# Gate sums, bank reads and first loads around the matmuls of a two-layer graph attention kernel

## The chip, the cores and the metric

The kernel runs on one core of a Trainium2 chip. The metric is device time in microseconds (us), lower is better. PE is the matmul engine, DVE the vector engine, ACT the scalar engine, POOL the general engine, SP the engine that issues most transfers. A "group" is four graphs; there are 32 groups in each of two layers, and they are counted here from 0 to 63.

Names in the traces: `xn` is a group's rows as loaded, `xT` the same rows turned (transposed), `T` POOL's sums of `xT`; `wv`, `wq`, `wk`, `wo` are weights with their sums; `e` is exp(scores), `av` the product of v and e; `aT` and `T_o` are the attention's result, turned, and its sums; `h` is the output before it is stored.

## The reference, cut to what matters

```python
# layer 0, per graph of N = 128 nodes, D = 512, 8 heads; everything is float32
Q, K, V = x @ W_q + b_q, x @ W_k + b_k, x @ W_v + b_v
scores  = Q K^T / sqrt(64) + (a_i + c_j + b_g) + log(adjacency + 1e-9)   # a, c = x @ halves of w_g: the gate sums
x1      = softmax(scores) V + x
# ... x1 is cut and turned into the graphs of layer 1
# layer 1: the same attention without the gate, then
h   = (attention output) @ Wo + bo + x1
out = layer_norm(h) * gamma + beta
```

The kernel never adds the logarithm: it multiplies exp(scores) by the turned adjacency. That product, `e <- e,adjT`, is DVE's largest job: 349.9 us in the trace before.

## The kernel before

Each 512 x 512 product is computed with Strassen's seven products P1 to P7; P2 is itself split by Strassen into four phases (P2.1 to P2.4) from the second group on. A matrix takes seven slots. Matrix n+1 starts while the last units of matrix n ("b") still run:

```python
SLOTS = ("P1", "P2.1"), ("P4 b",), ("P3 b", "P2.2"), ("P6", "P2.3"), ("P5",), ("P7", "P2.4"), ()
```

P2's phases share one PSUM bank, p1, with the next matrix. DVE must have read P2.4 out of p1 before PE may begin the next P2.1:

```python
def inner(phase):                       # P2's phases; DVE reads bank p1 after each
    ...
    else:                               # phase 4, after P7
        add(0, 0, p, v, 1, 3)           # DVE: last read of p1
def unit(i):
    ...
    elif i == "P7":
        kept("u3", p, 1, 1)             # ACT copies P7 out of its bank
        add(1, 1, t["b"], t["u3"])      # DVE adds it, ahead of the last read of p1
```

The rest of the work is hung on slots; `first` is the first slot of the group's matrix v, `put(post, ...)` issues behind the slot's matmuls.

```python
for k, i in enumerate((0, 0, 2, 6, 13, 17, 18, 19)):      # eight gate sums on DVE
    put(post, first + i, gate, t, k // 2, k % 2)
put(post, first + 20, gate_exp, t)
for k in range(2):
    put(post, first + 21 + k, add_row, t, k)               # bias row onto xn, on POOL
# start: xn whole on SP's queue, wv on ACT's queue; four turned graphs, then the sums of wv
for b in range(G):
    transposed(XT[0][:, b], XN[0, b // 2][:, b % 2], ...)   # copies out on ACT, DVE, ACT, DVE
Strassen.combine_outer(nc.vector, WV[0][0])                 # four additions and a negation of wv
# layer 1, end of a group: normalise on ACT, times gamma, plus beta on POOL, store from SP's queue
engine.tensor_tensor(HS[t, n], HS[t, n], wide(BE), ALU.add)
nc.sync.dma_start(out[...], HS[t, n])
```

(Cut: the loads, the attention, the path for unusual inputs, the last group, which works graph by graph.)

## Time and profile before

| | before |
|---|---|
| median of 4 runs | 3261.0 us (3260.05 to 3262.13) |
| span of the profiled run | 3259.4 us |
| PE busy | 3212.7 us, 99% |
| period of a group in layer 0 / layer 1 | 44.44 / 55.79 us |
| last scores to end of span | 44.1 us |

The prediction below shows the lines of the profile and reads them. To read on one needs one habit: a line's first number is its start, the second its duration, and what stands in brackets is how long its engine stood idle before it and for whom. For PE, start to start of the same step is a better measure than the durations: in the trace before, sixteen matmuls at 815.68 are shown 1.90 us long, and the next begin 1.73 us after them. In layer 1 a single group's period can lie up to 1.7 us above the common one, so I read sums over many groups.

### The profile page before, as it was taken

To read this page: it belongs to the slowest core of one execution; us is meant where nothing else is said; L and a number is where in the kernel's file an instruction comes from. 1 tells how busy PE (TensorE), PEld (TensorE's weight loads), DVE (VectorE), ACT (ScalarE), POOL (GpSimd) and SP (SyncE) were. 2 spreads that over 40 slices of the span, in tenths; PEclk is the share of its full clock that TensorE was granted. 3 is DMA by queue.
4 is the path that set the end of the run, shared out by engine and by line. 5 is a ranking of instruction groups with operands and counts; after the bars stand their busy time and mean duration, and the time that the engine had idled before them with its cause. 6 is when DMAs were issued, how large, how long until landed. Compare 5 with 4: busy or idle time off the path is not lost.

```text
span 3259.4 us, 95184 instructions
## 1 busy us (share of the span) xinstructions
PE 3212.7 (99%) x39974; PEld 2358.3 (72%) x39974; DVE 2023.1 (62%) x4070; ACT 1133.6 (35%) x1951; POOL 1806.0 (55%) x1518
## 2 busy tenths in 40 slices
PE   9999999999999999999999999999999999999997
PEld 6777777777777777776777777777777777777774
DVE  6777766777766777764555555555555555555555
ACT  2333333333333333333333333333333333333332
POOL 4444433444433444475676766576676757676765
PEclk9999999999999999999999999999999999999999
DMA  5333333333333333342343434343433334343432
GB/s 124 83 78 83 77 84 67 82 79 82 77 83 68 83 79 82 90 114 46 74 91 75 93 71 97 67 94 69 85 81 75 90 74 93 72 96 70 98 63 72
DMA packets 1017180, 265.82 MB, mean 82 GB/s; under 512 B 942640, under 2 KB 949808, under 8 KB 1016752
## 3 DMA queue, kind: packets, MB, share of 16 engines
q1 hardware_dynamic: 1015408, 258.39, 35.4%
q8 instruction: 319, 5.23, 0.7%
q10 hardware_dynamic: 1088, 1.05, 0.1%
q14 instruction: 109, 0.89, 0.1%
q0 software_dynamic: 256, 0.26, 0.0%
HBM read 159.92 MB, written 67.11 MB: 70 GB/s over the span
## 4 chain that ended last, share of the span: by engine, by line
PE 90%; DVE 5%; SPq 2%; issue 2%; DMA 1%; ACT 0%; POOL 0%; DVEq 0%; ACTq 0%
PE p0q L124 10%; PE p3v L124 9%; PE p3k L124 9%; PE s L124 8%; PE av L124 7%; PE p2v L124 7%; PE p2q L124 7%; PE p0o L124 6%; PE p2k L124 5%; PE p3q L124 3%; PE p2o L124 3%; PE p1v L124 3%; PE p1q L124 3%; PE p0k L124 3%; PE p1k L124 3%; DVE gw L124 2%
## 5 line engine op out<-in xcount | busy, mean ns | idle before, releaser
L124 DVE TENSOR_TENSOR e<-e,adjT 128x1024 f32<-128x1024 f32 x256 | 349.9, 1408 | 144.1 <-ACT e L124 144.1
L124 POOL TENSOR_TENSOR xn<-o,xn 128x1024 f32<-128x1024 f32 x64 | 140.9, 2202 | 455.0 <-DVE o L124 359.4
L124 POOL TENSOR_TENSOR xn<-xn,row 128x1024 f32<-128x1024 f32 x128 | 331.8, 2603 | 13.0 <-DMA xn<-x1d 10.0
L124 DVE SCALAR_TENSOR_TENSOR gw<-xn,gw 128x512 f32<-128x512 f32 x256 | 317.0, 1238 | 1.2
L124 PE MATMUL p3k<-T,wk 128*64 128x256 f32 x2256 | 268.5, 380 | 0.0
L124 PE MATMUL p0q<-T,wq 128*64 128x256 f32 x2256 | 267.4, 379 | 0.0
L124 PE MATMUL p3v<-wv,T 128*64 128x256 f32 x2256 | 267.4, 379 | 0.0
L124 POOL TENSOR_TENSOR T<-xT 128x512 f32<-128x512 f32 x128 | 219.3, 1713 | 84.5 <-DVE xT L124 83.9
L124 POOL TENSOR_TENSOR inner<-xT 128x128 f32<-128x128 f32 x126 | 67.5, 536 | 355.6 <-DMA adjT<-in_adj_dram 241.7
L124 PE MATMUL s<-qT,kT 64*128 64x128 f32 x4096 | 263.1, 278 | 0.0
L124 PE MATMUL av<-v,e 128*64 128x65 f32 x8192 | 260.9, 221 | 0.0
L124 PEld LDWEIGHTS av<-v,e 128*64 128x64 f32 x8192 | 256.6, 137 | 1.0 <-issue 0.8
L124 PEld LDWEIGHTS s<-qT,kT 64*128 64x128 f32 x4096 | 238.6, 188 | 22.4 <-issue 11.7
L124 POOL TENSOR_TENSOR h<-h,gamma 128x1024 f32<-128x1024 f32 x61 | 145.0, 2376 | 128.3 <-ACT h L124 128.2
L124 PEld LDWEIGHTS p3k<-T,wk 128*64 128x64 f32 x2256 | 159.5, 138 | 68.8 <-issue 1.3
L124 PEld LDWEIGHTS p0q<-T,wq 128*64 128x64 f32 x2256 | 159.1, 137 | 67.6
L124 PEld LDWEIGHTS p3v<-wv,T 128*64 128x64 f32 x2256 | 159.0, 137 | 67.7
L124 ACT COPY o<-av 128x520 f32<-128x520 f32 x256 | 151.7, 593 | 130.9 <-PE av L124 116.3
L124 POOL TENSOR_TENSOR h<-h,xn 128x1024 f32<-128x1024 f32 x62 | 146.8, 2390 | 62.1 <-ACT h L124 59.2
L124 DVE STREAM_TRANSPOSE xT<-xT 128x512 f32<-128x512 f32 x252 | 176.5, 701 | 0.5 <-issue 0.5
L124 PE MATMUL p0o<-wo,T_o 128*64 128x256 f32 x1488 | 176.4, 379 | 0.0
L124 DVE TENSOR_TENSOR t1q<-p1q,t1q 128x128 f32<-128x128 f32 x189 | 54.5, 288 | 188.5 <-PE p1q L124 187.4
(229 smaller groups left out, 6643.4 us busy)
## 6 DMA issues: line engine op xcount, KB each, us to landing
xn<-in_x_dram SPq DMA_DIRECT2D x64, 512.0 KB, 4.1
x1d<-xn SPq DMA_DIRECT2D x64, 512.0 KB, 3.0
xT<-x1d SPq DMA_DIRECT2D x512, 64.0 KB, 2.4
xn<-x1d SPq DMA_DIRECT2D x64, 512.0 KB, 6.1
xT<-in_x_dram SPq DMA_DIRECT2D x496, 64.0 KB, 2.6
out_dram<-h SPq DMA_DIRECT2D x62, 512.0 KB, 4.2
aT<-o SPq DMA_DIRECT2D x984, 32.0 KB, 2.0
adjT<-in_adj_dram SPq DMA_DIRECT2D x256, 64.0 KB, 3.5
```

The lines of the kernel that those rows point to most:

```text
L124: return lambda *args, **kw: self.tc.keep_in_program_order(f(*args, **kw))
```

## The change

Its intent: in layer 0, lay DVE's gate sums where POOL rests, so they do not hold up DVE (in the trace before they take 0.65 us at the least and up to 2.73 beside POOL); read p1 before U3 is added; at the start bring xn in quarters and wv over two queues and give PE something to do before; at the change of layers replace 16 matmuls for the output bias by eight weighted sums on DVE and move a turn of aT behind a read of p1; in the last group, work in pairs and let two groups' ends overlap.

```diff
             else:
                 add(0, 0, p, v, 1, 3)
+                add(1, 1, t["b"], t["u3"])
             elif i == "P7":
                 kept("u3", p, 1, 1)
-                add(1, 1, t["b"], t["u3"])
+                if not inside:
+                    add(1, 1, t["b"], t["u3"])
-            for k, i in enumerate((0, 0, 2, 6, 13, 17, 18, 19)):
+            for k, i in enumerate((6, 6, 10, 10, 13, 13, 21, 21)):
-                put(post, first + 21 + k, add_row, t, k)
+                put(post, first + (11, 22)[k], add_row, t, k)
-    load_natural(0)
-    strassen_weights(WV, 0, w_v0, "wv0", nc.scalar)
+    load_natural(0, nc.sync, nc.scalar)
+    strassen_weights(WV, 0, w_v0, "wv0", nc.sync, nc.scalar)
+    (eight matmuls of ones into a free bank)
     for b in range(G):
         transposed(...)
+        if b == 0:
+            Strassen.combine_outer(nc.vector, WV[0][0], 0)     # S1, S2: ahead of DVE's copies
-    Strassen.combine_outer(nc.vector, WV[0][0])
-    put(post, V2 + 17, output_bias)                           # 16 matmuls in the trace
+    put(post, V2 + (10, 10, 13, 13)[c], weigh_rows, c)        # on DVE
+    put(pre, V2 + 17, output_bias)                            # 4 in the trace, against ones
-                turned = f + 18
+                turned = f + (18 if t > NG else 21)
```

(Cut: three slots of the turns and one of the inner sums of xT, one slot of the gates' exponential, the later halves of the sums of wv and wq at the start, the steps of five slots at the change of layers, the last count's move into this list, and the last group's list.)

More of the change, by code (lines that the diff above doesn't have):

```diff
@@ L66, in load, with combine @@
     @staticmethod
-    def load(engine, t, w):
+    def load(engines, t, w):
         q = w.rearrange("(k c p) (m e) -> k m p c e", k=2, p=P, m=2)
-        for (k, m), i in Strassen.RAW.items():
-            engine.dma_start(t[:, i], q[k, m])
+        for n, ((k, m), i) in enumerate(Strassen.RAW.items()):
+            engines[n % len(engines)].dma_start(t[:, i], q[k, m])
     @staticmethod
-    def combine(v, a11, a12, a21, na22, s1, s2, s4):
-        v.tensor_tensor(s1, a21, na22, ALU.add)
-        v.tensor_tensor(s2, s1, a11, ALU.subtract)
+    def combine(v, a11, a12, a21, na22, s1, s2, s4, part=None):
+        if part != 1:
+            v.tensor_tensor(s1, a21, na22, ALU.add)
+            v.tensor_tensor(s2, s1, a11, ALU.subtract)
+        if part == 0:
+            return
         v.tensor_tensor(a21, a11, a21, ALU.subtract)
@@ L82, in combine_outer @@
     @staticmethod
-    def combine_outer(v, t):
+    def combine_outer(v, t, part=None):
         w = Strassen
-        w.combine(v, *(t[:, i] for i in (w.A11, w.A12, w.S3, w.NA22, w.S1, w.S2, w.S4)))
+        w.combine(v, *(t[:, i] for i in (w.A11, w.A12, w.S3, w.NA22, w.S1, w.S2, w.S4)), part)
     @staticmethod
@@ L124, in __getattr__, with fast_path @@
             return lambda *args, **kw: self.tc.keep_in_program_order(f(*args, **kw))
-def fast_path(ctx, tc, args, GOOD):
+def fast_path(ctx, tc, args, GOOD, bad):
     (x, adj, w_q0, b_q0, w_k0, b_k0, w_v0, b_v0, w_g, b_g, w_q1t, b_q1, w_k1t, b_k1, w_v1t, b_v1,
@@ L191, in load, with load_natural @@
             load_graph(t, b, nc.sync)
-    def load_natural(t):
+    def load_natural(t, *engines):
         L, g = split(t)
@@ L197, in load_natural @@
             XN[t, k] = act.tile([P, 2, D], F32, tag="xn", name=f"xn_{t}_{k}", bufs=4)
-            nc.sync.dma_start(XN[t, k], src[2 * k : 2 * k + 2].rearrange("b p d -> p b d"))
+            if not engines:
+                nc.sync.dma_start(XN[t, k], src[2 * k : 2 * k + 2].rearrange("b p d -> p b d"))
+            for b, engine in enumerate(engines):
+                engine.dma_start(XN[t, k][:, b], src[2 * k + b])
     def turn(v):
@@ L516, in stats, with root @@
         nc.vector.bn_aggr(MV[t][:, b], st)
+    def root(t, bs):
+        rs = RS[t][:, 0, bs]
+        nc.gpsimd.tensor_scalar_add(rs, MV[t][:, bs, 1], LN_EPS)
+        nc.gpsimd.tensor_tensor(rs, rs, minus_half[:, bs], ALU.pow)
     def scales(t, bs):
+        root(t, bs)
         mv, rs = MV[t][:, bs], RS[t][:, :, bs]
-        nc.gpsimd.tensor_scalar_add(rs[:, 0], mv[:, :, 1], LN_EPS)
-        nc.gpsimd.tensor_tensor(rs[:, 0], rs[:, 0], minus_half[:, bs], ALU.pow)
         nc.gpsimd.tensor_tensor(rs[:, 1], mv[:, :, 0], rs[:, 0], ALU.mult)
@@ L536, in store, with weigh_rows, strassen_weights @@
         )
-    def output_bias():
-        p = ps.tile([P, 4 * N], F32, tag="p2", name="pbo").rearrange("p (m e) -> p m e", m=2)
-        for m in range(2):
-            for c in range(KC):
-                nc.tensor.matmul(
-                    p[:, m], bvcols[:, c], WO[1][0][:, Strassen.RAW[c // 2, m], c % 2],
-                    start=(m == 0 and c == 0), stop=(c == KC - 1), skip_group_check=True,
-                )
-        r = ROWS[1].rearrange("p (m e) -> p m e", m=2)
-        nc.vector.tensor_tensor(r, p, r, ALU.add)
-    def strassen_weights(to, key, w, name, engine):
+    def weigh_rows(c):
+        for m in range(2):
+            o, w, b = GW[:, 2, m * D2 : (m + 1) * D2], WO[1][0][:, Strassen.RAW[c // 2, m], c % 2], bv1[:, c : c + 1]
+            if c == 0:
+                nc.vector.tensor_scalar(o, w, b, None, ALU.mult)
+            else:
+                nc.vector.scalar_tensor_tensor(o, w, b, o, op0=ALU.mult, op1=ALU.add)
+    def output_bias():
+        p = ps.tile([P, 2, D], F32, tag="s", name="pbo", bufs=2)[:, 0]
+        for half in HALVES:
+            nc.tensor.matmul(p[half], ones[:, half], GW[:, 2], start=True, stop=True, skip_group_check=True)
+        nc.vector.tensor_tensor(ROWS[1], p, ROWS[1], ALU.add)
+    def strassen_weights(to, key, w, name, *engines):
         to[key] = (
@@ L555, in strassen_weights @@
         )
-        Strassen.load(engine, to[key][0], w)
+        Strassen.load(engines, to[key][0], w)
     def combine(engine, w):
@@ L562, in fast_path @@
     load_tiles(0)
-    load_natural(0)
-    strassen_weights(WV, 0, w_v0, "wv0", nc.scalar)
+    load_natural(0, nc.sync, nc.scalar)
+    strassen_weights(WV, 0, w_v0, "wv0", nc.sync, nc.scalar)
+    ones = const.tile([P, P], F32, name="ones")
+    nc.vector.memset(ones, 1.0)
+    busy = ps.tile([P, 4 * N], F32, tag="p0", name="busy")
+    for i in range(4):
+        nc.tensor.matmul(busy[:, 0:N], ones, ones, start=True, stop=True)
     load_adjacency(0, nc.sync)
@@ L578, in fast_path @@
     for b in range(G):
-        transposed(XT[0][:, b], XN[0, b // 2][:, b % 2], f"x_{b}", nc.vector.tensor_copy if b % 2 else nc.scalar.copy, ("p1", "p2")[b % 2])
+        transposed(XT[0][:, b], XN[0, b // 2][:, b % 2], f"x_{b}", nc.vector.tensor_copy if b % 2 else nc.scalar.copy, ("p1", "p2", "p3")[b % 3])
+        if b == 0:
+            Strassen.combine_outer(nc.vector, WV[0][0], 0)
     TS[0] = quarters(XT[0])
-    Strassen.combine_outer(nc.vector, WV[0][0])
     for s in Strassen.SUMS:
@@ L599, in fast_path @@
     BQ[1], BK[1], bv1 = column(nc, const, b_q1, "bq1"), column(nc, const, b_k1, "bk1"), column(nc, const, b_v1, "bv1")
-    bvcols = GW[:, 3].rearrange("p (c e) -> p c e", e=P)
     GA, BE = row(nc, const, gamma, "gamma"), row(nc, const, beta, "beta")
@@ L633, in fast_path @@
         a = slot("k", t, 7)
-        for k in range(2):
-            put(pre, a + (4, 11 if t + 1 < LAST else 9)[k], scores, t, k)
+        step = 5 if t == NG else 7
+        for k in range(2 if t + 1 < LAST else 0):
+            put(pre, a + 4 + step * k, scores, t, k)
             for b in (2 * k, 2 * k + 1):
-                put(pre, a + (4, 11 if t + 1 < LAST else 9)[k], weigh, t, b)
+                put(pre, a + 4 + step * k, weigh, t, b)
             if t + 1 < LAST:
-                put(pre, a + 7 + 7 * k, mix, t, (2 * k, 2 * k + 1))
-                put(post, a + 7 + 7 * k, normalise, t, k)
+                put(pre, a + 7 + step * k, mix, t, (2 * k, 2 * k + 1))
+                put(post, a + 7 + step * k, normalise, t, k)
                 if L == 1:
-                    put(post, a + 8 + 7 * k, move, t, k, [nc.sync, nc.gpsimd] if t == NG and k else [nc.sync])
+                    put(post, a + 8 + step * k, move, t, k, [nc.sync, nc.gpsimd] if t == NG and k else [nc.sync])
         if t + 1 < LAST:
@@ L650, in fast_path @@
                 put(post, first + (-1 if t == 0 else 2 + 7 * (b // 2) * late), load_graph, n, b, nc.sync)
-                put(post, first + ((9, 13, 16, 17), (16, 17, 23, 24))[late][b], lambda n, b: turn(XT[n][:, b]), n, b)
+                put(post, first + ((8, 9, 15, 17), (16, 17, 23, 24))[late][b], lambda n, b: turn(XT[n][:, b]), n, b)
             put(post, first + (11, 16 if t == NG + 1 else 13)[late], load_adjacency, n, nc.sync)
@@ L654, in fast_path @@
             put(post, first + (13, 17)[late], lambda n: TS.update({n: quarters(XT[n])}), n)
-            put(post, first + (13, 17)[late], lambda n: inner_sums(TS[n], n), n)
+            put(post, first + (17, 17)[late], lambda n: inner_sums(TS[n], n), n)
             for s in Strassen.SUMS:
@@ L660, in fast_path @@
                 put(post, first + 17, load_natural, t + 1)
-            for k, i in enumerate((0, 0, 2, 6, 13, 17, 18, 19)):
+            for k, i in enumerate((6, 6, 10, 10, 13, 13, 21, 21)):
                 put(post, first + i, gate, t, k // 2, k % 2)
-            put(post, first + 20, gate_exp, t)
+            put(post, first + 21, gate_exp, t)
             for k in range(2):
-                put(post, first + 21 + k, add_row, t, k)
+                put(post, first + (11, 22)[k], add_row, t, k)
         else:
@@ L682, in fast_path @@
                     put(post, o + 1 + k, residual, t, k)
-                    stat, scaled, end, stored = (
-                        ((2, 6), 6, 9, 10), ((9, 10), 10, 13, 14)
-                    )[k] if t < LAST - 2 else (((3, 3), 3, 4, 5), ((6, 6), 6, 6, 7))[k]
+                    if t == LAST - 2:
+                        continue
+                    stat, scaled, end, stored = (((2, 6), 6, 9, 10), ((9, 10), 10, 13, 14))[k]
                     for b in range(2):
@@ L690, in fast_path @@
                         put(post, o + end, scale, t, 2 * k + b)
-                    put(post, o + stored, store, t, k, nc.vector if t == LAST - 2 and k else nc.gpsimd)
+                    put(post, o + stored, store, t, k, nc.gpsimd)
     V1, V2 = slot("v", NG - 1, 0), slot("v", NG, 0)
@@ L701, in fast_path @@
     put(post, V2 + 10, load_row, 1, b_o1)
-    put(post, V2 + 10, nc.vector.tensor_copy, bvcols, bv1.rearrange("p (c o) -> p c o", o=1).to_broadcast([P, KC, P]))
-    put(post, V2 + 17, output_bias)
+    for c in range(KC):
+        put(post, V2 + (10, 10, 13, 13)[c], weigh_rows, c)
+    put(pre, V2 + 17, output_bias)
     put(post, V2 + 18, lambda: Strassen.combine_outer(nc.gpsimd, WO[1][0]))
     put(post, slot("o", NG, 1), lambda: Strassen.combine_inner(nc.gpsimd, *WO[1]))
-    put(post, 2, lambda: Strassen.combine_outer(nc.vector, WQ[0][0]))
+    put(post, 0, lambda: Strassen.combine_outer(nc.vector, WV[0][0], 1))
+    put(post, 3, lambda: Strassen.combine_outer(nc.vector, WQ[0][0]))
     put(post, 7, turn_adjacency, 0)
@@ L714, in fast_path @@
     t = LAST - 1
-    a = slot("k", t, 11)
+    a = slot("k", t, 7)
     last = {}
@@ L747, in output_one, with begin_one @@
         stats(t, b)
-        rs = RS[t][:, 0, b : b + 1]
-        nc.gpsimd.tensor_scalar_add(rs, MV[t][:, b, 1:2], LN_EPS)
-        nc.gpsimd.tensor_tensor(rs, rs, minus_half[:, b : b + 1], ALU.pow)
-    def finish_one(b):
+        root(t, slice(b, b + 1))
+    def begin_one(t, b):
         h = HS[t, b // 2][:, b % 2]
-        nc.vector.tensor_scalar(h, h, MV[t][:, b, 0:1], RS[t][:, 0, b : b + 1], ALU.subtract, ALU.mult)
-        nc.vector.tensor_tensor(h, h, GA, ALU.mult)
-        nc.vector.tensor_tensor(h, h, BE, ALU.add)
+        nc.vector.scalar_tensor_tensor(h, h, MV[t][:, b, 0:1], GA, op0=ALU.subtract, op1=ALU.mult)
@@ L757, in finish_one @@
+    def finish_one(t, b):
+        h = HS[t, b // 2][:, b % 2]
+        nc.vector.scalar_tensor_tensor(h, h, RS[t][:, 0, b : b + 1], BE, op0=ALU.mult, op1=ALU.add)
         nc.sync.dma_start(out[split(t)[1] * G + b], h)
-    put(post, slot("v", t, 11), plain_weight)
-    put(post, a, prepare)
-    for b, i in enumerate((3, 4, 7, 8)):
-        put(pre, a + i, mix, t, (b,))
-        put(post, a + i, normalise_one, b)
-        put(pre, a + i + 2, transpose_one, b)
-        put(pre, a + i + 3, output_one, b)
-        put(post, a + (9, 9, 11, 12)[b], finish_one, b)
@@ L767, in fast_path, with store_one, sum_good @@
-    put(post, a + 9, count, t)
+    def store_one(t, b):
+        h = HS[t, b // 2][:, b % 2]
+        nc.gpsimd.tensor_tensor(h, h, GA, ALU.mult)
+        nc.gpsimd.tensor_tensor(h, h, BE, ALU.add)
+        nc.sync.dma_start(out[split(t)[1] * G + b], h)
+    def sum_good():
+        good = small.tile([P, 1], F32, name="good_sum", bufs=1)
+        nc.vector.tensor_reduce(good, GOOD, AX.X, ALU.add)
+        last["good"] = ps.tile([P, 4 * N], F32, tag="p1", name="good_total")[0:1, 0:1]
+        nc.tensor.matmul(last["good"], good, ones[:, 0:1], start=True, stop=True)
@@ new lines, in judge @@
+    def judge():
+        nc.vector.tensor_scalar(bad, last["good"], 2 * B * H * P - 0.5, None, ALU.is_lt)
+    put(post, slot("v", t, 11), plain_weight)
+    put(post, a + 4, prepare)
+    u = t - 1
+    for i, f, *of in (
+        (4, scores, t, 0), (4, weigh, t, 0), (4, weigh, t, 1), (8, mix, t, (0, 1)), (9, normalise_one, 0),
+        (9, normalise_one, 1), (9, scores, t, 1), (9, weigh, t, 2), (9, weigh, t, 3), (10, transpose_one, 0),
+        (10, transpose_one, 1), (11, stats, u, 0), (11, stats, u, 1), (11, output_one, 0), (11, scales, u, slice(0, 2)),
+        (12, mix, t, (2, 3)), (12, scale, u, 0), (12, scale, u, 1), (12, store_one, u, 0), (13, normalise_one, 2),
+        (13, normalise_one, 3), (13, stats, u, 2), (13, stats, u, 3), (13, output_one, 1), (13, store_one, u, 1),
+        (14, transpose_one, 2), (14, transpose_one, 3), (14, begin_one, t, 0), (14, finish_one, t, 0),
+        (14, begin_one, u, 2), (14, begin_one, t, 1), (14, finish_one, t, 1), (15, output_one, 2),
+        (15, root, u, slice(2, 4)), (15, begin_one, t, 2), (15, begin_one, u, 3), (15, finish_one, t, 2),
+        (16, output_one, 3), (16, begin_one, t, 3), (16, count, t), (16, sum_good), (16, finish_one, u, 2),
+        (16, finish_one, t, 3), (16, finish_one, u, 3), (16, judge),
+    ):
+        put(pre, a + i, f, *of)
@@ L797, in count_good @@
     )
-def any_bad(ctx, tc, GOOD, n, bad):
-    nc = tc.nc
-    pool = ctx.enter_context(tc.tile_pool(name="sums", bufs=1))
-    ps = ctx.enter_context(tc.tile_pool(name="sums_ps", bufs=1, space=PSUM))
-    good = pool.tile([P, 1], F32, name="sums_good")
-    nc.vector.tensor_reduce(good, GOOD, AX.X, ALU.add)
-    ones = pool.tile([P, 1], F32, name="sums_ones")
-    nc.vector.memset(ones, 1.0)
-    total = ps.tile([1, 1], F32, name="sums_total")
-    nc.tensor.matmul(total, good, ones, start=True, stop=True)
-    nc.vector.tensor_scalar(bad, total, n - 0.5, None, ALU.is_lt)
 def general_path(ctx, tc, args):
@@ L951 @@
     with ExitStack() as inner:
-        fast_path(inner, tc, args, GOOD)
-    with ExitStack() as inner:
-        any_bad(inner, tc, GOOD, 2 * B * H * P, bad)
+        fast_path(inner, tc, args, GOOD, bad)
     again = nc.values_load(
```

## The prediction

> **What bounds the kernel now.** I read the page first, then the table of who waited for whom for the matmul engine, then the starts of its instructions in order of time.
>
> ```profile
> PE 3212.7 (99%) x39974; PEld 2358.3 (72%) x39974; DVE 2023.1 (62%) x4070; ACT 1133.6 (35%) x1951; POOL 1806.0 (55%) x1518
> PEclk9999999999999999999999999999999999999999
> ```
> PE is busy 99% of the span at full clock, so a change that leaves the matmuls as they are can win only the moments in which PE stands still. Of 3259.4 us the page leaves 3259.4 - 3212.7 = 46.7 us. A gain of 2% would be 65 us, so it is nearly ruled out before any detail. The waits of PE say where those moments are:
>
> ```profile
> PE p1v L124 <- DVE kT L124: 13.4, 31, 0.8
> PE po L124 <- ACT aT_last L124: 6.5, 4, 4.4
> PE sums_total L810 <- DVE sums_ones L808: 5.9, 1, 5.9
> PE tr_x L124 <- DMA xn<-in_x_dram: 5.7, 1, 5.7
> PE p1o L124 <- DVE kT L124: 3.4, 1, 3.4
> ```
> The first row is one wait per group of four graphs in layer 0; the rest are single events at the end, the start and the change of layers. The waits understate it, because a matmul's end in the trace is modelled. Starts are better. The same step (P1 into one bank, then P2's first part into bank p1), once in matrix q and once in matrix v:
>
> ```profile
> 815.68 1.90 PE L124 MATMUL p3q<-xT,wq 128*64 128x256 f32 x16
> 817.41 0.61 PE L124 MATMUL p1q<-xT,wq 128*64 128x128 f32 x8
> 817.85 0.39 PE L124 MATMUL p1q<-inner,wq0i 128*64 128x128 f32 x4
> ...
> 843.46 1.90 PE L124 MATMUL p3v<-wv,xT 128*64 128x256 f32 x16
> 845.77 0.66 PE L124 MATMUL p1v<-wv,xT 128*64 128x128 f32 x8 [0.41 <-DVE kT L124]
> 846.25 0.39 PE L124 MATMUL p1v<-wv0i,inner 128*64 128x128 f32 x4
> ```
> In q the step lasts 817.41 - 815.68 = 1.73 us and then 0.44; in v it lasts 2.31 and then 0.48. So 0.58 + 0.04 = 0.62 us are lost, not 0.41. In each group v's later steps lose 0.12 more: P6 to the next part of P2 takes 1.80 for 1.73 and the step before the scores 0.37 for 0.32. Sum 0.74 us a group. What holds p1:
>
> ```profile
> 843.01 1.76 DVE L124 SCALAR_TENSOR_TENSOR gw<-xn,gw 128x512 f32<-128x512 f32 x1
> 844.18 1.72 POOL L124 TENSOR_TENSOR T<-xT 128x512 f32<-128x512 f32 x1
> 844.70 0.68 DVE L124 TENSOR_TENSOR kT<-p2k,u3k 128x512 f32<-128x512 f32 x1
> 845.30 0.41 DVE L124 TENSOR_TENSOR kT<-p1k,t1k 128x256 f32<-128x256 f32 x1
> ```
> A gate sum that takes 0.65 us when POOL rests takes 1.76 beside POOL's sums. Behind it DVE adds U3 (which first had to come through ACT), and only then reads P2's last part out of p1. PE may write p1 again at 845.77.
>
> The change of layers and the end:
>
> ```profile
> 1463.17 3.72 PE L124 MATMUL pbo<-wo,gw 128*128 128x256 f32 x16
> 1467.73 1.95 PE L124 MATMUL p2k<-T,wk 128*64 128x256 f32 x16 [0.84 <-DVE row L124]
> ...
> 1515.46 1.90 PE L124 MATMUL p0o<-wo,aT 128*64 128x256 f32 x16
> 1520.74 2.58 PE L124 MATMUL p1o<-wo,aT 128*64 128x256 f32 x16 [3.38 <-DVE kT L124]
> 1523.10 3.00 PE L124 MATMUL p3k<-T,wk 128*64 128x256 f32 x16
> ```
> ```profile
> 3241.70 5.40 PE L124 MATMUL po<-wo_plain,aT_last 128*128 128x512 f32 x8 [4.39 <-ACT aT_last L124]
> ...
> 3253.28 0.15 DVE L811 TENSOR_SCALAR bad<-sums_total 1x1 int32<-1x1 f32 x1 [0.44 <-PE sums_total L810]
> ```
> From DVE's last instruction (3253.43) to the end of the span lie 6.0 us that the chain does not shorten.
>
> [...]gate sums take 0.65 us alone, 1.76 to 2.73 beside POOL, while sums that read PSUM keep 0.68 beside it. [...]after the 3.4 us wait at 1520.74 the granted clock is 0.50 from 1522 to 1525. [...]
>
> **The change, part by part.** PE's order of matmuls is the same but for five places, found by comparing the two built programs; DVE's, POOL's and ACT's orders differ in every group.
>
> *Layer 0.* Gate sums go to slots 6, 6, 10, 10, 13, 13, 21, 21, in pairs where POOL rests, and P2's last read moves ahead of U3's addition. P2's last part ends about 0.3 us (PE to DVE, from 823.68 to 823.97) before DVE can read; then 0.41 us; p1 is free some 0.75 us after PE's last matmul in it, and PE needs it after 1.73. All 0.74 us should go: 31 x 0.74 = 22.9, and two of the 31 lose 0.34 more: 23.6. Against it: adding the bias row to half of xn now starts on POOL just as DVE weighs e. [...]DVE's pair (2 x 1.1) then ends at 6.7, and PE needs the second at 5.93 + 0.93 - 0.11 = 6.75. Nearly no margin; I take 1.5 us for it. Part: -22.
>
> *Layer 1.* The swap alone. At q to k and k to o the step takes 1.79 and 0.49 for 1.73 and 0.44 (2236.26 to 2238.05 to 2238.54, for one). Summed over all groups the excess is 2.37 + 1.67 + 1.97 + 1.58 = 7.6; part: -7.
>
> *Change of layers.* The output bias was 16 matmuls and a wait, 1467.73 - 1463.17 = 4.56 us; it becomes 8 half-width passes of 512 columns, each twice the 0.108 us of one of 256 columns (1.73 / 16), so 0.9: -3.6. The eight weighted sums that replace it lie on DVE. The late turn of aT held P2's read: 5.28 us for 1.73, and at half clock 2.36 and 2.83 for 1.73 each, 5.3 lost in all. Now the turn stands behind that read. The last aT transfer is no earlier in PE's time (the SP queue issues 16, then 8 of xT, then 8, 0.65 us each), so T2 is ready about 1.45 us after P6 wants it[...]: -3.8. A wait of 1.1 us at 1446.91 stays and gets a turn in front: +0.3. Part: -7.
>
> *Start.* xn comes in quarters on two queues, so PE can start near 4.0 rather than 5.68. But DVE now has two additions of wv ahead of its first copy of xT, and their data is the last quarter of the first 2 MB, which at the 250 to 340 KB each us seen here lands near 8.6. The copies end near 11.3, POOL's T2 near 14, and P6 starts there: 13.78 before. Behind it a wait of 0.46 at 24.65 goes, and 0.2 at 51.68. Part: -0.5.
>
> *End.* Transposes in pairs, all `po` at 0.46 us a pass without the 4.39 us wait. PE then ends po at about 3238.6, and DVE binds: from 3231.6, ten additions or products of 0.7 us, [...]two reads of po with statistics (1.5 each), the count (0.6), two last products. That gives 3246.2 for DVE's last, for 3253.43 before. Part: -7.
>
> Sum: 22 + 7 + 7 + 0.5 + 7 = 43.5; 3260.2 - 43.5 = 3216.7.
>
> **The rivals.** First: PE's wait only moves, in layer 0 from p1 to e[...]. For it: the margin of 0.05 us. Against: in layer 1 pairs of e of up to 4.39 us, ending 6.65 after the scores, cost PE nothing. At 0.3 us a group it would take 9 us: 3225. Second: only the waits as listed come back (13.4 + 3.4 + some of the end), the rest of the starts' excess being pipeline; then some 25 us: 3235. Against: layer 1's v takes 1.73 and 0.43 in the same step with nothing waiting. Third: the first wv additions before the copies hold the start longer than I think, +3 us. Fourth: transfers of h or aT that now come due earlier take the won time (two such waits, 1.5 and 0.5 us, are in the trace); 1 to 3 us.
>
> **Range and chances.** Errors by part: layer 0 4, layer 1 2, change 2.5, start 1.5, end 2.5 us; together about 6. Surprises mostly cost, so I lean up: 3217, 8 times in 10 within 3209 to 3227. Faster by over 2% needs 3195 or less: 2 in 100. Slower by 2% has nothing behind it: 1 in 100.
>
> **What would show it.** Right: the row "p1v <- DVE kT" gone, starts of layer 0's groups 43.7 us apart for 44.44, layer 1's steps at 1.73, pbo about 0.9 us, no second of clock 0.50 near the change, DVE's last instruction about 7 us nearer to the last scores. Wrong: a new row "av <- DVE e" with 31 entries, p0o or p2o waiting for POOL's T_o by more than 3 us, the first P6 later than 15 us[...].

## The result, and the profile after

| | before | after | ratio of fast runs |
|---|---|---|---|
| median | 3261.0 us | 3223.5 us (3223.03 to 3224.07, 4 runs) | 0.9885 (0.9868 to 0.9902) |
| span of the profiled run | 3259.4 us | 3221.2 us | |

A ratio is the mean time of one kernel's fast runs over that of the other's fast runs in the same rounds, so not quite the ratio of the medians.

To see where the time came from, I cut both traces at the same four points: P1 of matrix v in groups 2, 32 and 34, and the last scores.

| stretch | before | after | difference | predicted |
|---|---|---|---|---|
| start, to group 2 | 87.62 | 90.20 | +2.6 | -0.5 |
| layer 0, groups 2 to 32 | 1333.85 | 1312.01 | -21.8 | -22 |
| change of layers, groups 32 to 34 | 115.53 | 109.42 | -6.1 | -7 |
| layer 1, to the last scores | 1678.26 | 1672.43 | -5.8 | -7 |
| end | 44.14 | 37.14 | -7.0 | -7 |
| sum | 3259.4 | 3221.2 | -38.2 | -43.5 |

The busy line of the page after, to hold against the one in the prediction:

```profile
PE 3195.2 (99%) x39970; PEld 2373.5 (74%) x39970; DVE 1980.2 (61%) x4075; ACT 1131.3 (35%) x1949; POOL 1729.1 (54%) x1518
```

POOL's time fell by 1806.0 - 1729.1 = 77 us and DVE's by 43 us with nearly the same number of instructions, so they are shorter on average: POOL's bias rows take 2426 ns for 2603, its sums `T<-xT` 1507 for 1713. DVE's gate sums and its products with e, before and after (number, total us, mean ns):

```profile
L124 DVE SCALAR_TENSOR_TENSOR gw<-xn,gw 128x512 f32<-128x512 f32 x256 | 317.0, 1238 | 1.2
L124 DVE TENSOR_TENSOR e<-e,adjT 128x1024 f32<-128x1024 f32 x256 | 349.9, 1408 | 144.1 <-ACT e L124 144.1
```
```profile
L128 DVE SCALAR_TENSOR_TENSOR gw<-xn,gw 128x512 f32<-128x512 f32 x256 | 177.8, 695 | 4.4
L128 DVE TENSOR_TENSOR e<-e,adjT 128x1024 f32<-128x1024 f32 x256 | 420.5, 1682 | 139.7 <-ACT e L128 139.1
```

The gate sums lose 139 us and e gains 71: half of what the gate sums won moved to e, where it costs PE little (1.8 us in layer 0, measured in e4). The table of PE's waits after (total us, number, longest):

```profile
PE good_total L128 <- DVE good_sum L128: 5.2, 1, 5.2
PE p0v L128 <- DVE xT L128: 2.4, 1, 2.4
PE av L128 <- DVE e L128: 2.1, 3, 1.3
PE p1o L128 <- DVE h L128: 2.0, 5, 0.8
PE tr_o L128 <- ACT aT_last L128: 1.8, 2, 1.1
PE p0o L128 <- POOL T_o L128: 1.5, 1, 1.5
```

The row "p1v <- DVE kT" with its 31 entries is gone. New are a wait for xT, which is the start, and three for e at the change of layers. For h in layer 1 there are five waits where there were two, 2.0 us in all both times. The step that the prediction measured as 2.31 and 0.48 us, in the trace after (PE, then DVE):

```profile
833.74 1.90 PE L128 MATMUL p3v<-wv,xT 128*64 128x256 f32 x16
835.46 0.61 PE L128 MATMUL p1v<-wv,xT 128*64 128x128 f32 x8
835.90 0.39 PE L128 MATMUL p1v<-wv0i,inner 128*64 128x128 f32 x4
```
```profile
833.95 0.42 DVE L128 TENSOR_TENSOR kT<-p1k,t1k 128x256 f32<-128x256 f32 x1 [0.95 <-PE p1k L128]
834.45 0.69 DVE L128 TENSOR_TENSOR kT<-p2k,u3k 128x512 f32<-128x512 f32 x1
```

The step takes 1.72 and 0.44 us. DVE stands waiting for PE when P2's last part is done, reads it at once and adds U3 behind it; before, it came out of a gate sum of 1.76 us. The start is where the change lost. PE, then DVE, after:

```profile
8.54 1.98 PE L128 MATMUL p0v<-wv,xT 128*64 128x256 f32 x8 [0.80 <-DMA wv<-in_L_gnn_W_v_dram]
12.87 1.97 PE L128 MATMUL p0v<-wv,xT 128*64 128x256 f32 x8 [2.36 <-DVE xT L128]
14.63 2.66 PE L128 MATMUL p1v<-wv,xT 128*64 128x256 f32 x16
17.12 1.89 PE L128 MATMUL p0v<-wv,T 128*64 128x256 f32 x16
```
```profile
10.80 1.42 DVE L128 TENSOR_TENSOR wv<-wv 128x512 f32<-128x512 f32 x2 [9.79 <-DMA wv<-in_L_gnn_W_v_dram]
12.13 1.28 DVE L128 COPY xT<-tr_x 128x512 f32<-128x512 f32 x2
```

DVE stood still for 9.8 us, because the additions of wv are first in its order, and the third of wv's four quarters, the last that they need, landed at 10.70. Only behind them come the two copies of xT that PE and POOL wait for. The first P6, at 13.78 before, starts at 17.12. At the change of layers the trace after shows the shorter bias and the new waits:

```profile
1441.26 1.03 PE L128 MATMUL pbo<-gw,ones 128*64 128x512 f32 x4
1442.12 1.90 PE L128 MATMUL p0k<-T,wk 128*64 128x256 f32 x16
...
1464.42 1.15 PE L128 MATMUL av<-v,e 128*64 128x65 f32 x32 [1.34 <-DVE e L128]
...
1501.77 1.95 PE L128 MATMUL p0o<-wo,T_o 128*64 128x256 f32 x16 [1.51 <-POOL T_o L128]
```

The bias takes 1442.12 - 1441.26 = 0.86 us for 4.56. At the end, DVE's last instruction:

```profile
3215.05 0.14 DVE L128 TENSOR_SCALAR bad<-good_total 1x1 int32<-1x1 f32 x1
```

From the start of the last scores (3184.06) that is 31.1 us; before, 3253.43 - 3215.26 = 38.2. From 3193.43 on DVE stands still only twice for more than 0.2 us, 0.46 us each time, so it sets the end, as predicted.

### The profile page after: what moved, and what is told of

The parts are those of the page before. It is cut to its first block, busy times and chain, and to the rows that moved or that the text cites. A ratio compares the mean times of both kernels' runs of the same rounds, so it can differ in the third digit from the quotient of the medians.

```text
span 3221.2 us, 95065 instructions
## 1 busy us (share of the span) xinstructions
PE 3195.2 (99%) x39970; PEld 2373.5 (74%) x39970; DVE 1980.2 (61%) x4075; ACT 1131.3 (35%) x1949; POOL 1729.1 (54%) x1518
## 4 chain that ended last, share of the span: by engine, by line
PE 94%; SPq 2%; DVE 1%; DMA 1%; POOL 0%; issue 0%; ACT 0%; DVEq 0%; ACTq 0%; POOLq 0%
PE p3v L128 10%; PE p0q L128 10%; PE p3k L128 9%; PE s L128 8%; PE av L128 7%; PE p2v L128 7%; PE p2q L128 7%; PE p2k L128 6%; PE p0o L128 6%; PE p0k L128 4%; PE p0v L128 3%; PE p3q L128 3%; PE p2o L128 3%; PE p1v L128 3%; PE p1q L128 3%; PE p1k L128 3%
## 5 line engine op out<-in xcount | busy, mean ns | idle before, releaser
L128 DVE TENSOR_TENSOR e<-e,adjT 128x1024 f32<-128x1024 f32 x256 | 420.5, 1682 | 139.7 <-ACT e L128 139.1
L128 POOL TENSOR_TENSOR xn<-xn,row 128x1024 f32<-128x1024 f32 x128 | 310.4, 2426 | 159.1 <-DVE gw L128 151.9
L128 POOL TENSOR_TENSOR h<-h,gamma 128x1024 f32<-128x1024 f32 (+1 forms) x62 | 144.8, 2335 | 136.2 <-ACT h L128 136.2
L128 POOL TENSOR_TENSOR T<-xT 128x512 f32<-128x512 f32 x128 | 192.9, 1507 | 29.0 <-DVE xT L128 27.8
L128 DVE SCALAR_TENSOR_TENSOR gw<-xn,gw 128x512 f32<-128x512 f32 x256 | 177.8, 695 | 4.4
L128 ACT ACTIVATE e<-s,c 128x1024 f32<-128x1024 f32 x128 | 135.7, 1111 | 44.2 <-PE s L128 44.2
```

Source lines behind the costliest of these rows:

```text
L128: return lambda *args, **kw: self.tc.keep_in_program_order(f(*args, **kw))
```

## The experiments

Twelve runs, each with five rounds. The ratio is to the kernel before in the same rounds; the changed kernel's is 0.9885 or, as control e5, 0.9889.

### e1 to e3: what the start costs, order or loads

The rivals for the start: DVE's order (additions before copies), or the loads (wv lands later from two queues). e1 changes the order alone, e2 the loads alone, e3 both.

```diff
 e1 and e3
     for b in range(G):
         transposed(...)
-        if b == 0:
-            Strassen.combine_outer(nc.vector, WV[0][0], 0)
+    Strassen.combine_outer(nc.vector, WV[0][0], 0)
 e2 and e3
-    load_natural(0, nc.sync, nc.scalar)
-    strassen_weights(WV, 0, w_v0, "wv0", nc.sync, nc.scalar)
+    load_natural(0)
+    strassen_weights(WV, 0, w_v0, "wv0", nc.scalar)
```

> The changed kernel with one edit: DVE's two copies of xT stand before the two first additions of wv instead of behind the first transpose. Theory A (the additions wait for wv's last quarter and hold the copies behind them): copies near 8 to 9 us, POOL's T2 near 11.8, first P6 at 12.5 to 13.5 instead of 17.1, span 3.5 to 4.5 us shorter than 3223.5, so 3219 to 3220. Theory B (PE waits for the bytes of wv themselves, which land later from two queues): first P6 not earlier than 16 us, 3223 to 3224.

> The changed kernel with the loads of before (xn whole on one queue, wv on the other) but the new order of additions and copies. Theory A (order): the additions still stand before the copies and wait for wv, which lands at the earliest near 9.4 us; first P6 at 15.5 to 17, time 3222 to 3224. Theory B (loads): the start of before comes back, first P6 near 13.8, 3220.5 to 3221.5.

> The changed kernel with the loads of before and the copies first, so nearly the start of before. Both theories: first P6 near 13.8, 3220.5 to 3221.5. Against e1 it tells what the loads on two queues are worth once the order no longer hides it: about 1 us by theory A, nothing or a loss by theory B.

| | first P6 | group 1 starts | time | ratio |
|---|---|---|---|---|
| after | 17.12 | 46.48 | 3223.5 | 0.9885 |
| e1, copies first | 12.45 | 45.17 | 3223.3 | 0.9884 |
| e2, old loads | 14.26 | 43.67 | 3223.7 | 0.9889 |
| e3, both | 13.41 | 42.81 | 3223.0 | 0.9883 |

The first P6 did what theory A said for e1 and about what theory B said for e2, so each theory missed one run. The shorter times that were expected (3219 to 3220 for e1, 3220.5 to 3221.5 for e2 by theory B and for e3) all failed. With the old loads the additions can start much earlier, and the bad order costs only 14.26 - 13.41 = 0.85 us. DVE in e2:

```profile
8.82 1.42 DVE L128 TENSOR_TENSOR wv<-wv 128x512 f32<-128x512 f32 x2 [7.81 <-DMA wv<-in_L_gnn_W_v_dram]
10.15 1.28 DVE L128 COPY xT<-tr_x 128x512 f32<-128x512 f32 x2
```

They start at 8.82 for 10.80. The loss is therefore a product of both edits: on two queues wv landed about 2 us later, and the order makes everything else wait for it. Either edit undone repairs it. Landings vary: the start of the changed kernel gave a first P6 at 15.99 to 17.76 in four traces (after, e4 to e6), that of e1 12.45 and 13.68 (e1, e10), that of e3 13.41 to 14.18 (e3, e9, e11). The 0.85 us lies within this spread, the loss of both edits does not.

e1 then gave most of its 4.7 us back before group 1. PE in e1:

```profile
12.45 1.95 PE L128 MATMUL p0v<-wv,T 128*64 128x256 f32 x16 [0.65 <-DVE wv L128]
...
29.16 1.95 PE L128 MATMUL p2q<-T,wq 128*64 128x256 f32 x16 [2.67 <-DVE v L128]
```

DVE had a turn of the next group's xT in front of the addition to v, and that xT came late: SP's queue issues rows for layer 1 before it. In e10, where they are issued later, this wait of 2.67 us is gone. Here the earlier start met the next transfer sooner.

The larger surprise is the last two columns. The starts differ by up to 3.7 us at group 1, and no median differs. In the traces the won time is still there at group 34 in e2 (1508.88 for 1511.63) and gone at the last scores (3184.29 for 3184.06). It is lost in layer 1, a little in every second group: the sum of 28 groups (35 to 62) less 28 times the common period of 55.56 us is 3.8 us after, and 5.9, 6.8 and 7.3 us in e1 to e3. Below I call it layer 1's excess. It is not the same in each execution: one of four of e1, of e3 and of e4 took 3219.1 to 3219.5 us, less than any of the changed kernel, but the profiled ones took 3224 to 3225.

### e4: the bias row beside e

The prediction gave 1.5 us to POOL's bias row, which starts when two gate sums are done and then lies beside DVE's e. Exchanging two gate sums moves it.

```diff
-            for k, i in enumerate((6, 6, 10, 10, 13, 13, 21, 21)):
+            for k, i in enumerate((6, 6, 13, 13, 10, 10, 21, 21)):
-                put(post, first + (11, 22)[k], add_row, t, k)
+                put(post, first + (13, 22)[k], add_row, t, k)
```

> The changed kernel with the gate sums of graphs 1 and 2 exchanged, so that POOL's first bias row, which starts as soon as the sums of graphs 0 and 1 are done, falls behind DVE's weighing of e instead of beside it. Theory A[...]: the matmuls av of k=1 take 1.87 instead of 1.92 to 1.99 us in every group of layer 0 and 1.5 to 2.5 us are won, 3221 to 3222. Rival (the excess is pipeline, not e): av stays at 1.92 and more, 3223 to 3224. A second rival: the bias row now delays DVE's normalising or the next group's sums, and time is lost, 3225 or more.

The same place in both traces: DVE's e, then POOL's bias row, in the changed kernel

```profile
860.08 4.45 DVE L128 TENSOR_TENSOR e<-e,adjT 128x1024 f32<-128x1024 f32 x2 [0.21 <-ACT e L128]
```
```profile
859.95 2.37 POOL L128 TENSOR_TENSOR xn<-xn,row 128x1024 f32<-128x1024 f32 x1 [2.79 <-DVE gw L128]
```

and in e4:

```profile
859.26 2.36 DVE L128 TENSOR_TENSOR e<-e,adjT 128x1024 f32<-128x1024 f32 x2 [0.21 <-ACT e L128]
```
```profile
865.66 2.37 POOL L128 TENSOR_TENSOR xn<-xn,row 128x1024 f32<-128x1024 f32 x1 [9.31 <-DVE gw L128]
```

The pair of e takes 2.36 us for 4.45; the 2.1 us between them is nearly POOL's whole 2.37. Groups 2 to 32 take 1310.20 for 1312.01 us, so 1.8 us are won in layer 0: theory A, in which the bias row beside e delays it. (This stretch repeats well: it takes 1311.98 to 1312.07 us in after, e1 to e3, e5, e6 and e9, and 1310.20 in all three traces with the later bias row.) The time, 3222.6 us (3219.5 to 3225.2) at 0.9882, hardly shows it, because layer 1's excess was 7.0 us in the trace.

### e5 and e6: what takes the gains back in layer 1

The traces of the changed kernel and of e1 to e4 have PE waiting for DVE's h in layer 1, and DVE's h waiting for the store of the group before, because h has two buffers and each group uses both. e5 is the changed kernel once more as a control; e6 issues the stores from POOL's queue.

```diff
         engine.tensor_tensor(HS[t, n], HS[t, n], wide(BE), ALU.add)
-        nc.sync.dma_start(out[...], HS[t, n])
+        engine.dma_start(out[...], HS[t, n])
```

> The changed kernel unedited, once more, on the chip of its siblings in this call. In e1 to e4 the start or layer 0 became 1.3 to 3.7 us shorter in the traces, yet the span did not, because layer 1 lost 2 to 3 us more than in the first trace of the changed kernel. Theory C (layer 1 loses more on some chips: DVE's first write of h waits for the store of the group before, and its landing varies): this control shows an excess of layer 1 of 6 to 7 us as e1 to e4 do if it comes to the same chip, and 3225 to 3226. Rival (an earlier start itself makes layer 1 lose it again): an excess of 3.8 us, 3223 to 3224.

> The changed kernel with the stores of out issued from POOL's own queue, right behind POOL's product and sum, instead of from SP's queue, where they stand behind eight loads of xT. Theory C: the store is issued up to 3 us earlier, DVE's h no longer waits for it, PE's waits p1o <- DVE h are gone, layer 1's excess falls to 1 to 2 us: 2.5 to 5.5 us less than the control. Rival (the transfer itself is slow, or POOL's issue takes POOL's time from T_o and the sums): no gain, or 1 to 3 us lost to new waits for POOL.

The control took 3223.7 us (ratio 0.9889), e6 3219.5 us (0.9872). One group in the changed kernel: POOL's last work on the first half of h, SP's queue, then the waits of DVE and PE for that half's buffer:

```profile
1925.66 2.37 POOL L128 TENSOR_TENSOR h<-h,beta 128x1024 f32<-128x1024 f32 x1
```
```profile
1924.69 11.38 SPq L128 DMA_DIRECT2D aT<-o  x16
1936.12 5.36 SPq L128 DMA_DIRECT2D xT<-x1d  x8
1941.59 0.56 SPq L128 DMA_DIRECT2D out_dram<-h  x1
```
```profile
1946.93 0.29 DVE L128 TENSOR_TENSOR h<-p1o,t1o 128x128 f32<-128x128 f32 x1 [3.39 <-DMA out_dram<-h]
```
```profile
1947.37 0.44 PE L128 MATMUL p1o<-woi,inner_o 128*64 128x128 f32 x4 [0.78 <-DVE h L128]
```

This half of h is ready at 1925.66 + 2.37 = 1928.03, yet its store is issued at 1941.59, 13.6 us later, behind sixteen loads of aT and eight of xT; it lands at 1946.8 and PE loses 0.8 us. (The second half's store is the next one, at 1947.59.) The same group in e6, POOL and PE:

```profile
1926.00 2.37 POOL L128 TENSOR_TENSOR h<-h,beta 128x1024 f32<-128x1024 f32 x1
1928.66 0.81 POOL L128 DMA_DIRECT2D out_dram<-h  x1 [0.30 <-POOL h L128]
```
```profile
1946.75 0.39 PE L128 MATMUL p1o<-woi,inner_o 128*64 128x128 f32 x4
```

Issued 0.3 us after h is ready, and no wait. The expectation had the store up to 3 us earlier; it is 13 us earlier, so the 1.0 us that the transfer itself got shorter is not what ended the wait. Layer 1's excess falls from 4.9 us (control) to 0.4, the row "p1o <- DVE h" is gone, and the median from issue to landing of these stores falls from 4.6 to 3.6 us. The issue of the 24 loads in front took 16.8 us, the store waited 13.6 us for it ahead of a transfer of 5.2, and it was the part that mattered.

The control decided nothing between its theories: it came to another chip than e1 to e4, its time is the rival's, and its excess of 4.9 us is neither's; e7, on the control's chip, has 6.6. Its start came 1.1 us earlier than in the first trace (group 1 at 45.35 for 46.48) and layer 1 lost 1.1 us more, in the same code. What makes the stores cost 4 us in one trace and 7 in another stays open. That the late stores are the cause does not: e6 and e9 show it. By the cuts the control repeats layer 0 (-21.8), the change of layers (-6.1) and the end (-6.9).

### e7 and e8: which of the two edits carries layer 0

e7 puts the exchange of the two reads alone on the kernel before, e8 the slots of layer 0 alone (their diffs are the first two parts of the change).

> The kernel before with only the exchange of P2's last read and U3's addition. If exchange and placement are substitutes in layer 0 (either one alone makes p1 free in time): layer 0's group falls from 44.44 to 43.8 or 43.9, layer 1 by 6 us, in all 3235 to 3239. If they add up, each with about half of the 0.74 us: group 44.1, 3242 to 3246.

> The kernel before with only the other slots of layer 0 (gate sums, their exponential, the bias rows, the turns and inner sums of xT). Substitutes: layer 0's group 43.85 to 43.95, as the steps of layer 1 of before lose some 0.1 each, layer 1 unchanged at 55.79, in all 3242 to 3246. Additive: group 44.1, 3249 to 3252.

| groups 2 to 32 | us | against before |
|---|---|---|
| before | 1333.85 | |
| e7, exchange alone | 1333.36 | -0.5 |
| e8, slots alone | 1315.45 | -18.4 |
| after, both | 1312.01 | -21.8 |

The times are 3256.2 us (0.9984) and 3242.3 us (0.9942). Both of my alternatives failed for e7: the exchange alone is worth nothing in layer 0. The wait was moved. The waits of e7:

```profile
PE p1v L124 <- DVE t1v L124: 15.5, 30, 0.5
```

and the place, PE, DVE and POOL:

```profile
849.28 1.90 PE L124 MATMUL p3v<-wv,T 128*64 128x256 f32 x16
851.69 0.44 PE L124 MATMUL p1v<-wv,inner 128*64 128x128 f32 x4 [0.52 <-DVE t1v L124]
```
```profile
847.91 2.73 DVE L124 SCALAR_TENSOR_TENSOR gw<-xn,gw 128x512 f32<-128x512 f32 x1
```
```profile
847.34 5.51 POOL L124 TENSOR_TENSOR xn<-xn,row 128x1024 f32<-128x1024 f32 x2
```

P1 to P2.1 is now on time, but at P2.3 PE waits for DVE's read of p1 after P2.2, which stands behind a gate sum of 2.73 us beside POOL's bias rows: 851.69 - 849.28 = 2.41 us for 1.73. PE was early and paid at the next place where DVE was late. e8 came out as the alternative of substitutes has it: its gate sums take 694 ns on average, for 1238 before, and most of both waits is gone. Only then is the exchange worth its 3.4 us. Which of the moved slots does it (gate sums, bias rows, turns, inner sums) was not separated.

In layer 1 the exchange does what it should: e7's common period is 55.56 us for 55.79.

### e9 to e11: do the gains add up when the stores no longer take them

e9 is e6 with the start of e3. e10 takes e1, e4 and e6 and adds two edits; e11 is e10 with the old loads.

```diff
 e10 and e11, besides e1, e4, e6
-                put(post, first + 23 + k, add_row, t, k)
+                put(post, first + (23 if t > NG else 31) + k, add_row, t, k, nc.gpsimd if t > NG else nc.vector)
-    BQ[1], BK[1], bv1 = ...; GA, BE = ...          # rows of layer 1, loaded before xT of group 1
+    put(post, 14, later_rows)
```

> e6 and e3 together: the stores on POOL's own queue, the loads of before and the copies ahead of the additions of wv. If the stores were what took the earlier start back, the start's 3.5 to 4.3 us (group 1 at 42.8 us instead of 46.5 or 47.1) now reach the end: 3215 to 3216.5. If something else in layer 1 absorbs an early start, 3219 to 3220 as e6.

> The changed kernel with the copies first (e1), the bias row later (e4), the stores on POOL's queue (e6), the first two bias rows of layer 1 on DVE where it rests instead of on POOL beside e, and the rows of layer 1 loaded behind the first xT instead of ahead of it. By the terms: 3219.5 of e6, less 3.5 to 5 for the start if the 2.7 us wait of e1 goes with the rows, less 1.8 for the bias row, less 1.5 for the wait av <- DVE e at the change of layers: 3211 to 3213. Rival: the waits move on (T_o at the change of layers, DVE in layer 0) and half of it stays: 3214 to 3217.

> e10 with the loads of before (xn whole on one queue, wv on the other). If loads on two queues are worth 1.3 us (copies of xT at 6.3 and 8.0 against 7.6 and 9.3 us in e1 and e3), 1 to 1.5 us over e10, 3212 to 3214.5; if not, within 0.5 us of e10.

| | time | ratio |
|---|---|---|
| e6 | 3219.5 | 0.9872 |
| e9 | 3216.0 | 0.9870 |
| e10 | 3212.9 (3211.2 to 3213.4) | 0.9859 |
| e11 | 3212.7 (3212.6 to 3213.3) | 0.9860 |

All three fell within what was expected, e11 in both of its ranges, which overlap. In e9 the earlier start, worthless in e3, reaches the end: in the traces group 2 starts at 86.87 us for 90.84 in e6, and the span is 3214.4 for 3218.4. The ratios of e6 and e9 do not show it; each is known to about 0.0016, the kernel before varying by itself (3254.8 to 3264.8 us in these rounds). e10 against the changed kernel by the same cuts: start -3.4, layer 0 -1.8, change of layers -1.5, layer 1 -3.4, end 0; sum -10.2 = 3211.0 - 3221.2. PE's waits in e10:

```profile
PE tr_o L128 <- ACT aT_last L128: 1.8, 2, 1.1
PE p0o L128 <- POOL T_o L128: 1.5, 1, 1.5
...
PE av L128 <- DVE e L128: 0.8, 2, 0.4
```

The 1.34 us for e at the change of layers is gone: the two bias rows that POOL had laid beside e are now on DVE, where it rests. With the copies first, loads on two queues (e10 against e11) are worth nothing measurable in time. e10 and e11 are the fastest of all, about 0.34% under the changed kernel by the medians, (3223.5 - 3212.7) / 3223.5, though on another chip, and 0.26% by the ratios, whose intervals overlap a little.

### e12: the change of layers and the end by themselves

The changed kernel with the old slots, the old reads and nearly the old start.

```diff
 e3's diff, and the first two parts of the change taken back
```

> The kernel before with only the change of layers (the bias as eight sums on DVE, the turn of aT later, steps of five) and the last group in their new form, nearly its own start, the old order in layers 0 and 1. If the two parts stand by themselves as the blind sum has it: layer 0's groups at 44.44, layer 1's at 55.79, 6 to 7 us won at the change of layers, 7 between the last scores and the end, so 3245 to 3248. If part of the end's gain came from an earlier DVE or from the exchange of the two reads, the stretch from the last scores to the end stays above 40 us and the time above 3250.

It took 3250.9 us (3248.2 to 3252.6, ratio 0.9973), outside the 3245 to 3248. By the cuts, against before: start +2.7, layer 0 -0.1, change of layers -5.8, layer 1 -1.5, end -6.9; sum -11.7 = 3247.7 - 3259.4 in the profiled run, one of the faster ones. Both parts stand by themselves as predicted, though a time above 3250 was the rival's number; its sign, over 40 us from the last scores to the end, is absent (37.2). The miss comes from my mixture: with the old slots, two gate sums that wait for their load stand ahead of additions of wv, and PE waits 2.8 us for these.

## Why the prediction was right or wrong, point by point

The time, 3223.5 us, lies in the range, 6.5 us above the middle, because one term had the wrong sign and two were somewhat large. Nor would a better start alone have shown in the time: e1 to e3 repaired it, and layer 1 took it back in most executions.

- **Layer 0, -22: right, -21.8.** The groups are 43.73 us apart. The margin for e, 0.05 us, was my estimate of when the pair of e ends beside the bias row, and it was judged well: the bias row costs 1.8 us (e4), predicted 1.5. What the prediction did not say is that the two edits are not alike: the slots carry it, and without them the exchange only moves the wait (e7, e8).
- **Layer 1, -7: -5.8.** The exchange gave 0.23 us in each of 29 groups, so 6.7. The term that was missing is the stores, which are issued late in both kernels: what the prediction listed as a small rival (two such waits in the trace before) made the excess 1.1 us larger than before, perhaps because PE now comes to h sooner. With the stores issued earlier the part is worth 9.2 (5.8 + 3.4, e10).
- **Change of layers, -7: -6.1.** The bias (-3.7 for -3.6) and the wait of 1.5 us for T_o came as worked out, and the clock did not fall (granted clock 1.00 in each stretch from 1490 to 1530). The bias's working holds a slip: eight passes of twice 0.108 us would take 1.73 us, not 0.9; the trace has four, and these take 0.86. The term that was missing: three waits for e, 2.1 us in all, the longest where the first bias rows of layer 1 on POOL lie beside e; e10 takes that one away and wins 1.5.
- **End, -7: right, -7.0,** with DVE as the bound; e12 repeats it alone with -6.9. The prediction's 3246.2 for DVE's last also allowed 2.4 us for POOL's work beside it, my estimate.
- **Start, -0.5: wrong, +2.6.** The failed step is the landing of wv, "near 8.6" at the rate of transfer of the trace before: the quarter that the additions need landed at 10.70, and they started at 10.80 (9.59 to 11.36 in the four traces with this start). PE's first transposes did start at 4.09 us for 5.68. From the additions on the chain is nearly as worked out: additions and copies took 2.6 us (2.7 in the prediction), and POOL's T2 ended at 16.18, 2.8 us behind them (2.7). A second term was missing. P6 came at 17.12 not behind T2 but behind PE's own steps, P1's second half and P2, which took 1.76 and 2.49 us for 0.87 and 1.73. In e6, with the same start, the granted clock was 0.53 from 13.60 to 15.50, and P2's matmuls took 616 ns in the median, for 379 in e2; the view of the trace after lists 1.00 there, so for that run the cause is not shown. This is the third rival, named with +3 us and taken too lightly, and the first P6 later than 15 us is one of the prediction's own signs of being wrong. The prediction saw the order, and got the input of the order wrong.
- **Rivals.** The first (the wait moves to e) did not come true as stated, with a row of 31 entries and 9 us; e cost 1.8 us in layer 0 (e4), about the 1.5 that the sum had allowed for it. The second (only the listed waits come back) fell: layer 0 gave 21.8 us where 13.4 were listed. The fourth (transfers take won time) came true through the stores, at 1 us here and up to 3.5 more in e1 to e4.

## What to carry to other kernels

Before moving an instruction ahead in an engine's order, ask when its last operand lands: here DVE waited 9.8 us for one, and the copies behind it ran at 12.13 where in e1 the first began at 6.26. A wait taken away where PE stands can show up at the next place where the same engine is late, as in e7 (-0.5 us in layer 0, with 30 waits for t1v, 15.5 us in all), so look for the engine that is late and not for the wait. Look also at what runs beside it: a gate sum of 0.69 us took 1.76 at one place beside POOL and 2.73 at another, and a pair of e 4.45 for 2.36. The listed waits are not the whole loss: 13.4 us were listed in layer 0, and 21.8 came back. When gains that the trace shows do not reach the end, look downstream for a buffer freed by a transfer, and at the queue in front of that transfer: match each store with the write that made it ready, since here the first of two waited 13.6 us, and with the stores on POOL's queue the kernel took 4.2 us less (e5 and e6).
